# Dividing the spare-bank products of an attention layer over two steps

## The chip, the cores and the metric

The kernel runs on one core of a Trainium2 chip. The metric is the device time of one execution in microseconds (us); the time of a kernel is the median of several runs. TensorE is called PE in the profile, VectorE DVE, ScalarE ACT, GpSimd POOL and SyncE SP.

## The reference

A graph-attention layer with residual normalization, in float32, on x of shape 8 x 2048 x 256 and a 2048 x 2048 adjacency matrix that is shared by all eight frames and all heads (8 heads of 32 channels):

```
q, k, v = split(x @ w_qkv)
scores  = where(adj > 0, q k^T / sqrt(32), -1e9)
t       = softmax(scores) @ v
y       = layernorm(x + t) * g1 + be1
h       = relu(y @ w1 + b1)
z       = layernorm(y + h @ w2 + b2) * g2 + be2
out     = layernorm(x + z)
```

## The kernel before

**Items.** The main loop (L513) goes over 8 frames x 4 query chunks (qc, 512 rows each) x 2 head groups (g, four heads each) x 16 key blocks (mb, 128 keys each): 1024 items. In what follows a frame is 128 steps of this loop, a group is the 16 steps of one (qc, g), and G0 to G7 are the groups of a frame. For each item the scores of four heads are formed transposed, with keys on the partitions (`scores`, L204 to L219): four float32 matmuls of 512 columns into two of three pairs of PSUM banks, then two VectorE additions of the mask (L218), each from one pair into half of an SBUF tile `p`. ScalarE takes exp in place (L222), PE sums values over the 16 key blocks in one PSUM bank (L234), and the denominators are gathered by GpSimd additions (L256) and accumulating DMAs (L253) of the `p` tiles, and by products with a matrix of ones (L292).

**Order.** The program order of every engine is written by hand; nothing is reordered afterwards. One pass t of the loop issues: fill work (`advance`, L526, not at mb 0), the exponentials of item t+1, the scores of item t+2, the values of item t, the additions of item t.

**Banks.** Eight PSUM banks: six in three pairs for scores, two (`ps_x`) that change sides with every group: one holds the running values, the other is the spare bank for fill work. All fill products and transposes inside the loop go through this one bank, each evicted by ScalarE or VectorE before the next may write.

**Fill work.** Everything else is written as Python generators that yield between pieces: the transposes of x and the query projections of a coming frame (`turn`, L155; `queries`, L142; through DRAM, since the transposed chunk is written to `XD` and reloaded later), the reload (`reload`, L177) and the K and V projections of a chunk (`project`, L186; `channels`, L169, makes one 128 x 512 projection of two matmuls with the contraction halved), the denominator of a group (L280), the division (`divide`, L321), and the tail (L333) with the feed-forward (L386) and two further normalizations (`norm`, L259).

A generator yields `BANK` when it wants the spare bank, a number n when it may go on n steps later, and other negative marks for other resources: input tiles (`INPUTS`, three tiles in turn, L110 to L119), the `turned` tile, and room for a tail (two at a time). `advance(t, 1)` (L428) goes over the entries of `fill`, sorted by due time (L422), and runs each one until it has to wait; one piece in a step gets the bank:

```
                if e[2] == BANK:
                    if not banks:
                        break
                    banks -= 1
```

The table `NEXT` (L453) says at which step of a frame the turns and projections of the following frame are started. A reload's `yield 3` (L183) leaves three steps between its DMA and its first product; a K projection waits until all K projections before it exist (L189). If the V of a coming item is missing, the loop L533 calls `advance` until it is there. After the last item the remaining generators are run one after the other (L543).

**Pieces that the change touches.** A projection of Q or K (L172, two matmuls of 512 columns), a value projection (L197, eight matmuls of 128 columns), a first feed-forward product (L405, two matmuls of 512 columns), a second one (L415, four matmuls of 256 columns), and the ones-product (L292), which already runs in two pieces, half of its terms in each, with a second `yield BANK` (L289) between them. Float32 matmuls appear in the profile as two instructions each.

Of the kernel before, what the change touches and what calls it, by code (L numbers as in the profile page):

```python
# [10 lines left out]
F32 = mybir.dt.float32  # L11
# [8 lines left out]
P = 128  # L20
H = 8
D = 32
CH = 512
# [3 lines left out]

SUM_MIN = 1e-25
SUM_MAX = 1e19
BANK, TURNED, ROOM, INPUTS = -1, -2, -3, -10  # L30

MASKED = -57344.0
CODE = -5.0
# [22 lines left out]
def fast_path(ctx, tc, cst, x, adj, out, RS):  # L56
    nc = tc.nc
    F, N, C = x.shape
    NCK, TPC, MB = N // CH, CH // P, N // P
# [17 lines left out]
    ctx.enter_context(tc.manual_schedule())  # L77

    ident, identb, wqkv, w1s, w2s = cst["ident"], cst["identb"], cst["wqkv"], cst["w1s"], cst["w2s"]
    state = {"pair": 0, "side": None, "turn": 0, "turned": False, "tails": 0}  # L80

    def score_pair():
        i = state["pair"]
# [55 lines left out]
    QT, KT, V, XT = {}, {}, {}, {}  # L139
    XD = [dp.tile([NCK, P, 2, CH], F32, name=f"xd{f}") for f in range(F)]  # L140

    def queries(f, c, xT):  # L142
        for g in range(2):
            yield BANK
            QT[f, c, g] = channels(qp, "qT", xT, g * P)

    def turn_rows(xc, xT):
        for a in range(2):
# [17 lines left out]
        yield from queries(f, c, xT)  # L166
        give(xT)

    def channels(pool, name, xT, k0):  # L169
        ps = bank()  # L170
        for a in range(2):
            nc.tensor.matmul(ps, wqkv[:, a, k0:k0 + P], xT[:, a, :], start=(a == 0), stop=(a == 1))  # L172
        t = pool.tile([P, CH], F32, name=name)
        nc.scalar.copy(t, ps)
        return t

    def reload(f, c):  # L177
        while (f, c) not in XT:
# [7 lines left out]
    def project(f, c, g, xT=None):  # L186
        if xT is None:
            xT = yield from reload(f, c)
            while len(KT) < (2 * f + g) * NCK + c:  # L189
                yield 1  # L190
        yield BANK
        KT[f, c, g] = channels(kp, "kT", xT, C + g * P)
        yield BANK
        ps = bank()
        for j in range(TPC):
            for a in range(2):
                nc.tensor.matmul(ps[:, j * P:(j + 1) * P], xT[:, a, j * P:(j + 1) * P],  # L197
                                 wqkv[:, a, 2 * C + g * P:2 * C + (g + 1) * P], start=(a == 0), stop=(a == 1))
        v = vp.tile([P, TPC, P], F32, name="v")
        nc.scalar.copy(v, ps.rearrange("p (j c) -> p j c", c=P))  # L200
        V[f, c, g] = v
        give(xT)
# [21 lines left out]
    LAST = MB - 1  # L224
# [55 lines left out]
    def denominator(f, qc, g):  # L280
        grp = (f, qc, g)
        terms = [PT.pop((f, qc, g, ALONE))] + [PT.pop((f, qc, g, chain[0])) for chain in MOVED + (POOLED,)]
        if (f, qc, g) == items[-1][:3]:
            terms[3:3] = [PT.pop((f, qc, g, b)) for b in ENDED]
        yield BANK
        ps = bank()
        for n, term in enumerate(terms):
            if n == 2:
                yield BANK  # L289
            for h in range(4):  # L290
                r = D * h
                nc.tensor.matmul(ps[r:r + D, :], cst["ones"], term[:, h, :], start=(n == 0), stop=(n == len(terms) - 1))  # L292
        dT = op.tile([P, CH], F32, name="dT")
        nc.scalar.copy(dT, ps)  # L294
        yield 1
        yield BANK
        ps = bank()
        for j in range(TPC):
            nc.tensor.transpose(ps[:, j * P:(j + 1) * P], dT[:, j::TPC], ident)
        if g == 0:  # L300
            RC[f, qc] = op.tile([P, TPC, H], F32, name="rc")
        rc = RC[f, qc]
        den = ps.rearrange("p (j c) -> p j c", c=P)[:, :, ::D]
        nc.vector.reciprocal(rc[:, :, 4 * g:4 * g + 4], den)
        nc.vector.tensor_tensor(RS[:, 0], RS[:, 0], den, ALU.add)
        nc.vector.tensor_tensor(RS[:, 1], RS[:, 1], den, ALU.min)
        if g == 1:
            begin = items.index((f, qc, g, LAST)) + SUM + 2
            start(begin, outcome(f, qc) if (f, qc) != (F - 1, NCK - 1) else finish(f, qc), begin)
# [76 lines left out]
    def feed_forward(y):  # L386
        yield TURNED
        state["turned"] = True
        yT = work.tile([P, 2, CH], F32, name="turned")
        for a in range(2):  # L390
            yield BANK
            ps = bank()
            for j in range(TPC):
                nc.tensor.transpose(ps[:, j * P:(j + 1) * P], y[:, j, a * P:(a + 1) * P], ident)  # L394
            nc.scalar.activation(yT[:, a, :], ps, AF.Identity, bias=cst["be1c"][:, a:a + 1], scale=cst["g1c"][:, a:a + 1])
        yield 1
        nc.gpsimd.tensor_tensor(y, y, rows(cst["g1r"]), ALU.mult)
        yield 1
        nc.gpsimd.tensor_tensor(y, y, rows(cst["be1b2r"]), ALU.add)
        hT = work.tile([P, 2, CH], F32, name="hT")  # L400
        for d in range(2):
            yield BANK
            ps = bank()
            for a in range(2):
                nc.tensor.matmul(ps, w1s[:, a, d * P:(d + 1) * P], yT[:, a, :], start=(a == 0), stop=(a == 1))  # L405
            nc.scalar.activation(hT[:, d, :], ps, AF.Relu, bias=cst["b1s"][:, d:d + 1], scale=1.0)
        state["turned"] = False
        yield 1
        z = y
        for jj in range(0, TPC, 2):  # L410
            yield BANK
            ps = bank()
            for j in range(jj, jj + 2):
                for d in range(2):
                    nc.tensor.matmul(ps[:, (j - jj) * C:(j - jj + 1) * C], hT[:, d, j * P:(j + 1) * P], w2s[:, d, :],  # L415
                                     start=(d == 0), stop=(d == 1))
            nc.vector.tensor_tensor(z[:, jj:jj + 2, :], ps.rearrange("p (b c) -> p b c", c=C), z[:, jj:jj + 2, :], ALU.add)
# [7 lines left out]

    def advance(t, banks):  # L428
        inputs = True
        for e in list(fill):  # L430
            while e[0] <= t:
                if e[2] == BANK:
                    if not banks:
                        break
                    banks -= 1
                elif e[2] < INPUTS:
                    inputs = inputs and not any(u is not None for u in live[:INPUTS - e[2]])
                    if not inputs:
                        break
                elif e[2] == TURNED and state["turned"] or e[2] == ROOM and state["tails"] == 2:  # L440
                    break
                e[2] = next(e[1], None)
                if e[2] is None:
                    fill.remove(e)
                    break
                if e[2] > 0:
                    e[0] = t + e[2]

    items = [(f, qc, g, mb) for f in range(F) for qc in range(NCK) for g in range(2) for mb in range(MB)]
    LEAD = 2  # L450
# [62 lines left out]
    for t, (f, qc, g, mb) in enumerate(items):  # L513
# [9 lines left out]
            state["rows"] = take([P, TPC, C], F32)  # L523
            nc.sync.dma_start(state["rows"], x[f, qc * CH:(qc + 1) * CH, :].rearrange("(p j) c -> p j c", p=P))
        if mb:
            advance(t, 1)  # L526

        if t + 1 < len(items):
            exponentials(items[t + 1])
        if t + LEAD < len(items):  # L530
            nf, _, ng, nmb = items[t + LEAD]
            t0 = t
            while (nf, nmb // TPC, ng) not in V:  # L533
                advance(t0, 1)
                t0 += 1
            scores(items[t + LEAD])
        values(items[t])
# [4 lines left out]
    state["side"] = None  # L542
    while fill:  # L543
        t += 1
        advance(t, 1)


@with_exitstack
# [233 lines left out]
```

## Time and profile before

| | us |
|---|---|
| median of 3 runs | 3436.56 (3432.72 to 3441.2) |
| the profiled execution's own time | 3440.89 |
| its span, first to last instruction | 3439.1 |
| PE busy | 3179.1 (92%) |
| VectorE busy | 2731.0 (79%) |
| GpSimd busy | 2586.7 (75%) |
| ScalarE busy | 2426.5 (71%) |
| first scores of the loop / last scores | 56.0 / 3377.7 after the start |

A line of the page's groups names the source line, the engine, the operation, what it writes and reads, the count, the busy time, the mean duration in ns, and the idle time of the engine before it with what ended it. A line of the timeline gives start, duration, engine, line and operation, `x8` for eight instructions merged, and in brackets the idle time before it. A line of the waits gives who waited for whom: total us, number of times, longest. PEld is PE's weight load. Ends of matmuls are modelled, starts are recorded. Tiles named `s` are the score pairs, `x` the two other banks, `p` the exponentials, `in` the input tiles, `xd` the transposed chunks in DRAM.

### The profile page before, as it was taken

To read this page: it belongs to the slowest core of one execution; us is meant where nothing else is said; L and a number is where in the kernel's file an instruction comes from. 1 tells how busy PE (TensorE), PEld (TensorE's weight loads), DVE (VectorE), ACT (ScalarE), POOL (GpSimd) and SP (SyncE) were. 2 spreads that over 40 slices of the span, in tenths; PEclk is the share of its full clock that TensorE was granted. 3 is DMA by queue.
4 is the path that set the end of the run, shared out by engine and by line. 5 is a ranking of instruction groups with operands and counts; after the bars stand their busy time and mean duration, and the time that the engine had idled before them with its cause. 6 is when DMAs were issued, how large, how long until landed. Compare 5 with 4: busy or idle time off the path is not lost. (4 is left out here: it accounts for less than half of the span.)

```text
span 3439.1 us, 54435 instructions
## 1 busy us (share of the span) xinstructions
PE 3179.1 (92%) x22036; PEld 1038.5 (30%) x22036; DVE 2731.0 (79%) x3203; ACT 2426.5 (71%) x1937; POOL 2586.7 (75%) x1357
## 2 busy tenths in 40 slices
PE   6989999999999999999999999999999999998995
PEld 5222332223322233222332323223332223322222
DVE  4788768887788877888788887888768887689885
ACT  3677767776677767777677776777767777677774
POOL 0577768887688776888678876787777877788885
PEclk8999999999999999999999999999999999999998
DMA  8678768778678777778777777687776787777774
GB/s 309 149 156 173 173 161 174 158 159 200 142 167 184 154 180 153 163 172 181 170 154 170 161 175 178 141 180 172 164 179 140 160 187 167 169 158 154 151 162 99
DMA packets 149298, 575.99 MB, mean 167 GB/s; under 512 B 14608, under 2 KB 67344, under 8 KB 99888
## 3 DMA queue, kind: packets, MB, share of 16 engines
q0 software_dynamic: 64560, 435.85, 63.2%
q1 hardware_dynamic: 83664, 135.30, 11.4%
q8 instruction: 174, 2.85, 0.3%
q10 hardware_dynamic: 816, 1.31, 0.1%
q14 instruction: 84, 0.69, 0.1%
HBM read 131.99 MB, written 37.75 MB: 49 GB/s over the span
## 5 line engine op out<-in xcount | busy, mean ns | idle before, releaser
L218 DVE TENSOR_TENSOR p<-s,mask 128x1024 f32<-128x1024 f32 x2048 | 2410.0, 1219 | 568.5 <-PE s L215 343.9
L222 ACT ACTIVATE p<-p 128x2048 f32<-128x2048 f32 x1024 | 1956.6, 1911 | 484.6 <-DVE p L218 371.2
L256 POOL TENSOR_TENSOR p<-p 128x2048 f32<-128x2048 f32 x382 | 1851.8, 4898 | 385.9 <-ACT p L222 383.4
L215 PE MATMUL s<-qT,kT 32*128 32x512 f32 x8192 | 1169.8, 641 | 184.9 <-DVE p L218 174.6
L234 PE MATMUL x<-p,v 128*32 128x512 f32 x8192 | 1091.8, 605 | 2.3 <-ACT p L222 2.3
L253 POOL DMA_DIRECT2D p<-p x384 | 385.6, 1024 | 376.0 <-DMA p<-p 188.4
L215 PEld LDWEIGHTS s<-qT,kT 32*128 32x128 f32 x8192 | 320.5, 183 | 822.3 <-DVE p L218 756.2
L234 PEld LDWEIGHTS x<-p,v 128*32 128x32 f32 x8192 | 161.1, 108 | 780.1 <-issue 211.5
L172 PE MATMUL x<-in,wqkv 128*128 128x512 f32 x472 | 235.2, 621 | 14.7 <-DMA in<-xd 14.1
L292 PE MATMUL x<-p,ones 128*32 128x512 f32 x2064 | 244.9, 592 | 1.9 <-DMA p<-p 1.9
L274 ACT ACTIVATE y<-y,nb,rs 128x256 f32<-128x256 f32 x372 | 219.0, 590 | 7.1 <-POOL nb L271 7.1
L263 DVE BATCH_NORM_STATS2 st<-y 128x6 f32<-128x256 f32 x372 | 155.4, 418 | 0.0
L172 PEld LDWEIGHTS x<-in,wqkv 128*128 128x128 f32 x472 | 80.2, 189 | 170.9 <-issue 112.7
L294 ACT COPY dT<-x 128x512 f32<-128x512 f32 x64 | 37.4, 585 | 126.3 <-PE x L292 126.3
L415 PE MATMUL x<-w2s,hT 128*128 128x256 f32 x504 | 125.5, 392 | 0.1
L405 PE MATMUL x<-turned,w1s 128*128 128x512 f32 x248 | 123.0, 618 | 0.0
L197 PEld LDWEIGHTS x<-wqkv,in 128*128 128x128 f32 x896 | 104.2, 191 | 47.0 <-issue 41.1
L197 PE MATMUL x<-wqkv,in 128*128 128x128 f32 x896 | 114.9, 281 | 0.0
L292 PEld LDWEIGHTS x<-p,ones 128*32 128x32 f32 x2064 | 66.8, 110 | 156.4 <-issue 151.0
L415 PEld LDWEIGHTS x<-w2s,hT 128*128 128x128 f32 x504 | 90.6, 189 | 62.0 <-issue 50.3
L268 POOL TENSOR_TENSOR rs<-rs,mhalf 128x4 f32<-128x4 f32 x93 | 96.2, 1035 | 7.8
L200 ACT COPY v<-x 128x512 f32<-128x512 f32 x58 | 33.9, 585 | 93.6 <-PE x L197 93.6
(114 smaller groups left out, 1467.6 us busy)
## 6 DMA issues: line engine op xcount, KB each, us to landing
p<-p POOLq DMA_DIRECT2D x384, 1024.0 KB, 10.1
mask<-md SPq DMA_DIRECT2D x248, 128.0 KB, 6.2
y<-in_x_dram POOLq DMA_DIRECT2D x62, 512.0 KB, 6.1
in<-xd SPq DMA_DIRECT2D x59, 512.0 KB, 10.9
p<-in_adj_dram SPq DMA_DIRECT2D x16, 1024.0 KB, 9.6
out_dram<-y SPq DMA_DIRECT2D x31, 512.0 KB, 6.4
in<-in_x_dram SPq DMA_DIRECT2D x29, 512.0 KB, 10.4
xd<-in SPq DMA_DIRECT2D x28, 512.0 KB, 9.2
```

The costliest lines, as they stand in the source:

```text
L172: nc.tensor.matmul(ps, wqkv[:, a, k0:k0 + P], xT[:, a, :], start=(a == 0), stop=(a == 1))
L197: nc.tensor.matmul(ps[:, j * P:(j + 1) * P], xT[:, a, j * P:(j + 1) * P], wqkv[:, a, 2 * C + g * P:2 * C + (g + 1) * P], start=(a == 0), s ...
L215: nc.tensor.matmul(ps2[half][:, j, :], KT[f, mb // TPC, g][r:r + D, (mb % TPC) * P:(mb % TPC + 1) * P], QT[f, qc, g][r:r + D, :], start=Tr ...
L218: nc.vector.tensor_tensor(pt[:, 2 * half:2 * half + 2, :], ps, MK[f, qc, mb // 2][:, mb % 2, None, :].to_broadcast([P, 2, CH]), ALU.add)
L222: nc.scalar.activation(PT[item], PT[item], AF.Exp, scale=1.0 / math.sqrt(D))
L234: nc.tensor.matmul(O[grp][r:r + D, :], V[f, mb // TPC, g][:, mb % TPC, r:r + D], PT[item][:, h, :], start=(mb == 0), stop=(mb == LAST))
L253: nc.gpsimd.dma_start(PT[f, qc, g, chain[0]], PT.pop(item), accum_op=ALU.add)
L256: nc.gpsimd.tensor_tensor(first, first, PT.pop(item), ALU.add)
L263: nc.vector.bn_stats(st, t[:, j, :])
L274: nc.scalar.activation(t[:, j, :], t[:, j, :], AF.Identity, bias=nb[:, j:j + 1], scale=rs[:, j:j + 1])
L292: nc.tensor.matmul(ps[r:r + D, :], cst["ones"], term[:, h, :], start=(n == 0), stop=(n == len(terms) - 1))
L415: nc.tensor.matmul(ps[:, (j - jj) * C:(j - jj + 1) * C], hT[:, d, j * P:(j + 1) * P], w2s[:, d, :], start=(d == 0), stop=(d == 1))
```

## The change

Projections, value projections and both feed-forward products get a new mark, `MORE`, in their middle. A job that has yielded `MORE` becomes the holder of the bank: the next call of `advance` resumes it first and gives the bank to nobody else. If, at the end of the call in which it stopped, another entry is due and waits for `BANK`, the holder is resumed at once, so that its product is issued whole. The calls at mb 15, in the loop that waits for a V, and after the last item finish the holder in any case. The ones-product's second `yield BANK` becomes `HOLD`, which keeps the bank for the next step whether others wait or not. `channels` becomes a generator that stores its result itself.

```diff
     def queries(f, c, xT):
         for g in range(2):
-            yield BANK
-            QT[f, c, g] = channels(qp, "qT", xT, g * P)
+            yield from channels(QT, qp, "qT", (f, c, g), xT, g * P)
...
-    def channels(pool, name, xT, k0):
+    def channels(store, pool, name, key, xT, k0):
+        yield BANK
         ps = bank()
         for a in range(2):
+            if a:
+                yield MORE
             nc.tensor.matmul(ps, wqkv[:, a, k0:k0 + P], xT[:, a, :], start=(a == 0), stop=(a == 1))
-        t = pool.tile([P, CH], F32, name=name)
-        nc.scalar.copy(t, ps)
-        return t
+        store[key] = pool.tile([P, CH], F32, name=name)
+        nc.scalar.copy(store[key], ps)
...
-        yield BANK
-        KT[f, c, g] = channels(kp, "kT", xT, C + g * P)
+        yield from channels(KT, kp, "kT", (f, c, g), xT, C + g * P)
         yield BANK
         ps = bank()
         for j in range(TPC):
+            if j == TPC // 2:
+                yield MORE
             for a in range(2):
...
             if n == 2:
-                yield BANK
+                yield HOLD
...
             for a in range(2):
+                if a:
+                    yield MORE
                 nc.tensor.matmul(ps, w1s[:, a, d * P:(d + 1) * P], yT[:, a, :], start=(a == 0), stop=(a == 1))
...
             for j in range(jj, jj + 2):
+                if j > jj:
+                    yield MORE
                 for d in range(2):
...
+    def resume(e, t):
+        e[2] = next(e[1], None)
+        state["holder"] = e if e[2] in (MORE, HOLD) else None if state["holder"] is e else state["holder"]
+        if e[2] is None:
+            fill.remove(e)
+        elif e[2] > 0:
+            e[0] = t + e[2]
+
-    def advance(t, banks):
+    def advance(t, free=True, finish=False):
         inputs = True
+        if state["holder"]:
+            free = False
+            resume(state["holder"], t)
         for e in list(fill):
-            while e[0] <= t:
+            while e[2] is not None and e[0] <= t and e is not state["holder"]:
                 if e[2] == BANK:
-                    if not banks:
+                    if not free:
                         break
-                    banks -= 1
+                    free = False
...
-                e[2] = next(e[1], None)
-                if e[2] is None:
-                    fill.remove(e)
-                    break
-                if e[2] > 0:
-                    e[0] = t + e[2]
+                resume(e, t)
+        late = any(e[2] == BANK and e[0] <= t for e in fill)
+        while state["holder"] and (finish or late and state["holder"][2] == MORE):
+            resume(state["holder"], t)
...
         if mb:
-            advance(t, 1)
+            advance(t, finish=mb == LAST)
...
             while (nf, nmb // TPC, ng) not in V:
-                advance(t0, 1)
+                advance(t0, finish=True)
                 t0 += 1
...
     while fill:
         t += 1
-        advance(t, 1)
+        advance(t, finish=True)
```

More of the change, by code (lines that the diff above doesn't have):

```diff
@@ L29 @@
 SUM_MAX = 1e19
-BANK, TURNED, ROOM, INPUTS = -1, -2, -3, -10
+BANK, MORE, HOLD, TURNED, ROOM, INPUTS = -1, -2, -3, -4, -5, -10
 MASKED = -57344.0
@@ L79, in fast_path @@
     ident, identb, wqkv, w1s, w2s = cst["ident"], cst["identb"], cst["wqkv"], cst["w1s"], cst["w2s"]
-    state = {"pair": 0, "side": None, "turn": 0, "turned": False, "tails": 0}
+    state = {"pair": 0, "side": None, "turn": 0, "turned": False, "holder": None, "tails": 0}
     def score_pair():
```

## The prediction

> **What bounds the kernel now.** I read the page first (busy shares, groups), then the timeline of single steps, then the waits and the DMA issues. "Step t" is one pass of the loop over items: fill work of L526, exponentials of item t+1, scores of t+2, values of t. There are 1024 (L222's count), 128 to a frame, in groups G0 to G7 of 16; "mb" is a step's place in its group.
>
> ```profile
> PE 3179.1 (92%) x22036; PEld 1038.5 (30%) x22036; DVE 2731.0 (79%) x3203; ACT 2426.5 (71%) x1937; POOL 2586.7 (75%) x1357
> ...
> L172 PE MATMUL x<-in,wqkv 128*128 128x512 f32 x472 | 235.2, 621 | 14.7 <-DMA in<-xd 14.1
> ...
> L415 PE MATMUL x<-w2s,hT 128*128 128x256 f32 x504 | 125.5, 392 | 0.1
> L405 PE MATMUL x<-turned,w1s 128*128 128x512 f32 x248 | 123.0, 618 | 0.0
> ...
> L197 PE MATMUL x<-wqkv,in 128*128 128x128 f32 x896 | 114.9, 281 | 0.0
> ```
>
> PE leads, but 92% is an average over two kinds of step. The counts give the products that use the spare bank inside the loop: 472/4 = 118 projections (L172), 248/4 = 62 first and 504/8 = 63 second feed-forward products, 896/16 = 56 value projections, 299 in all. First a step without fill work, in the timeline (start, length, then the idle time before it):
>
> ```profile
> 1473.41 1.14 PE L215 MATMUL s<-qT,kT 32*128 32x512 f32 x8 [0.41 <-DVE p L218]
> ...
> 1474.48 1.07 PE L234 MATMUL x<-p,v 128*32 128x512 f32 x8
> ...
> 1474.67 2.35 DVE L218 TENSOR_TENSOR p<-s,mask 128x1024 f32<-128x1024 f32 x2 [0.19 <-issue]
> 1475.95 0.31 PEld L215 LDWEIGHTS s<-qT,kT 32*128 32x128 f32 x8 [1.32 <-DVE p L218]
> 1475.95 1.14 PE L215 MATMUL s<-qT,kT 32*128 32x512 f32 x8 [0.41 <-DVE p L218]
> ```
>
> Scores to scores is 2.54 us. PE's own work is 1.07 (scores to values) plus 1.00 (values to whatever is next, 1507.71 to 1508.71 below), 2.07; the other 0.47 it waits for VectorE's mask add, which frees the pair that the next scores overwrite. Now a step with a whole projection:
>
> ```profile
> 1506.64 1.14 PE L215 MATMUL s<-qT,kT 32*128 32x512 f32 x8
> ...
> 1507.71 1.06 PE L234 MATMUL x<-p,v 128*32 128x512 f32 x8
> ...
> 1507.85 2.36 DVE L218 TENSOR_TENSOR p<-s,mask 128x1024 f32<-128x1024 f32 x2 [0.76 <-PE s L215]
> ...
> 1508.71 0.30 PEld L172 LDWEIGHTS x<-in,wqkv 128*128 128x128 f32 x2 [0.84 <-ACT y L274]
> 1508.71 1.98 PE L172 MATMUL x<-in,wqkv 128*128 128x512 f32 x4
> 1509.24 0.19 PEld L172 LDWEIGHTS x<-in,wqkv 128*128 128x128 f32 x1 [0.24 <-issue]
> 1509.67 0.19 PEld L172 LDWEIGHTS x<-in,wqkv 128*128 128x128 f32 x1 [0.24 <-issue]
> 1510.62 0.31 PEld L215 LDWEIGHTS s<-qT,kT 32*128 32x128 f32 x8 [0.76 <-DVE p L218]
> ```
>
> This one takes 3.98 us, PE never waits, and VectorE idles some 1.6. So PE bounds the full steps and the loop PE-VectorE the empty ones: 0.47 us of PE is unused in each empty step. Starts of the matmul groups, sorted over the whole loop, give 357 empty steps (median 2.544), 64 of them at mb 0, where no fill work is called. Two waits belong to single places:
>
> ```profile
> DVE y L417 <- POOL y L399: 22.3, 13, 3.7
> ...
> PE x L172 <- DMA in<-xd: 14.1, 8, 3.1
> ```
>
> **What the Trainium skill says.** "TensorE: Matmul & The Clock Gate", Part 3, The mechanism: matmuls start and end strictly in program order. The trace agrees: every step's groups start in the code's order, so a product put before the scores delays them by its length. "Perfetto Trace Analysis", Tensor Engine Instruction: the reported end of a matmul is an estimate. The trace agrees (1506.64 + 1.14 lies behind the next start, 1507.71), so I use starts alone. "PSUM — Partial Sum Buffer", The four PSUM rules: a matmul that opens a sum clears flags only in its own bank; an open sum can stay while others run in other banks. The ones-products (L288) already do so here at 3.78 us for each of their steps. "DMA: Bandwidth & Descriptors", Issuing engines are not separate DMA queues: SP's and GpSimd's transfers share 16 engines. It agrees: the 512 KB reload `in<-xd` lands 10.9 us after its issue in the median, but 3.2 to 16.9 us in single issues, shortest where no accumulating `p<-p` is under way.
>
> **The change, part by part.** *Price of one division.* In the full step PE's starts are 0.53, 0.43, 0.43 and 0.52 us apart (two passes to each matmul), 1.91 in all. A half is 0.53 + 0.52 = 1.05, so a divided pair of steps is 2 x (2.07 + 1.05) = 6.24 us against 3.98 + 2.54 = 6.52: **0.28 us gained**. L405 has the same starts, and L415 (0.32 + 2 x 0.216 + 0.31 a half) and L197 (0.21 + 6 x 0.112 + 0.20) come to 0.28 too. The half step needs cover: VectorE has 2.36 plus 0.65 where a row statistic falls in, 3.0 of 3.12; ScalarE 1.91 (exp) + 0.59 (eviction) + 0.59 (normalize) = 3.1, just full, but such steps come singly.
>
> *How many.* A job is divided only if no other one waits for the bank, and not at mb 15. I took the order of the fill jobs from the trace (frames 1 to 6 are alike) and walked it by hand under the new rule: C projection, V values, h and z the feed-forward's two, o ones, d/r/x/y transposes, + the second half of the job before it, a dot no fill work.
>
> ```
>      before            after                before            after
> G0   .zVoodrr........  .zzoodrrVC+VC+VC  G4 .zCoodrrV.......  .hzzoodrrV+.....
> G1   ...oodxxCCyy.hhz  .V+oodxxC+Cyy.h+  G5 ...oodxxCCyyChhz  ...oodxxC+CyyC+h
> G2   .z.oodrr........  .h+zzoodrr......  G6 .zVoodrrxxCCCVCV  .hzzoodrrxxCCV+.
> G3   ...oodxxCCyy.hhz  ...oodxxC+CyyC+h  G7 .CVoodCVCVyyChhz  .C+oodVC+VyyC+hh
> ```
>
> Most jobs stay whole because a second job is queued: the later z halves meet the waiting ones-product, the V's the next chunk's K. 15 per frame are divided; frame 0 has 13 (no tails yet), frame 7 has 10 (no projections of its own): 6 x 15 + 13 + 10 = **113**. Sum: 113 x 0.28 = **31.6 us less**. The rest of the empty steps stays empty (17 of 32 usable per frame).
>
> *What moves with it.* All jobs keep their work, but jobs slip by up to nine steps, with the evictions, row statistics and DMAs that follow them.
> - Second feed-forward product: today its eviction waits at mb 15 for GpSimd's additions (22.3 us of VectorE waits above); in trace steps G4 mb 0 is 0.86 us longer than an empty step and G6's 0.23. The product comes one to four steps later, the additions at most one. Gain about 1.1 a frame, 7 in all.
> - Row statistics after it (L263, 0.65 us each) slip from the ones steps, where VectorE idles, into d and r steps, where it is full (r steps are 0.11 over their PE length already). Up to 0.6 in each of G2, G4, G6 and 0.3 in G0, less 1.2 taken out of x steps and empty steps of G1, G3, G5: about +1 a frame, 7 in all, against the gain before it.
> - Reloads on SP's queue. Today the fourth chunk's K projection (G6 mb 14) waits 0 to 4.6 us, 2.2 on average, for its reload, which waits for its own write to DRAM; it now comes at G7 mb 7, with time to spare. In its place: the second chunk's V (due later than all others) moves from G6 mb 2 to mb 13 and 14 and holds its input tile till then, so the third chunk's reload, until now issued as early as G5 mb 15 to G6 mb 12, is issued only at its end. Its K projection starts two empty steps and one scores-values later, 0.2 + 2 x 2.54 + 2.07 = 7.4 us. At 7 to 11 us for a first reload in that stretch (8.1 to 10.6 for those issued at G6 mb 12) PE waits 0 to 3.6; I take 2. The first chunk's reload (issued G3 mb 8, landing after 15 to 17 us) is needed 15.2 us later: 0.6 more. Together +0.4 a frame; bounds -2 and +3, or -15 and +20 over seven frames. Behind PE's wait stand the scores and so all engines. The mask loads that SP has queued are for the next query chunk, not due.
> - ones-products slip by two steps in G2, one in G4 and G6; the `p` tiles they hold have 11 buffers and no wait of VectorE for GpSimd's sums shows.
> - The end (61 us after the last scores) is bound by the last sums and gets one second product more, 2 us beside their transfers: 0.
>
> These four shifts cancel to within about 10 us; I take 0. The profiled execution took 3440.9 us (span 3439.1, 1.8 around it), so 3409 for one like it; it was 4.3 above the median of the three runs. From the median: 3436.6 - 31.6 = **3405 us**.
>
> **Rivals.**
> A, *slower*: the third chunk's reload. If it lands S us after PE is ready, the time is 3405 + 7 x (S - 2); from S = 6.5 (a landing after 13.9 us) there is no gain. For it: other reloads take 13 to 17 us behind mask loads or as third in a row. Against: this one is first in the queue, with the last accumulation of its group ending. At 16 us S is 8.6 and the time 3451.
> B, *half steps are not PE-bound*: ScalarE's 3.1 us and VectorE's moved statistics make a pair 6.4 rather than 6.24: 113 x 0.14 = 16, time 3421. For it: both engines are within 4% of the half step. Against: only one in three halves carries such an extra.
> C, *hardly anything is divided*: if my walk misses waiting jobs and only the places with long empty runs behind them count (G1 to G4, about 50 in all): 14 us, time 3423.
> D, *all usable empty steps are filled*: 293 x 0.28 = 82, time 3355. Against: the queued jobs above; bursts and empty runs lie in different groups.
>
> **How the numbers follow.** Forecast 0.72, B 0.11, C 0.07, A 0.06, D 0.04. The forecast's own spread is about 12 us (reloads, statistics, 10 divisions more or fewer = 3 us, the median's own scatter of 4): 3393 to 3417. Up to 3426 it takes in B and C, and leaves A, D and the tails out: 3393 to 3426. About 0.3% (10 us) is what a measurement of this kernel can tell from no change, so faster means below 3426: 0.71 + 0.09 + 0.05 + 0.04 = 0.89, which I lower to 0.86 for what I have not seen; same 0.09; slower 0.05.
>
> **What would show it.** Right: about 113 pairs of steps at 3.12 us with two L172 or L405 passes each; some 113 fewer empty steps; L215's wait for L218 shorter; G6 mb 14 at 3.1 us with half a V; a wait `PE x L172 <-DMA in<-xd` at G7 mb 1 instead of G6 mb 14. Wrong: half steps above 3.2 us (B), far fewer divided products (C), or that DMA wait above 6 us a frame (A).

## The result, and the profile after

| | before | after |
|---|---|---|
| median of 4 runs each, side by side | 3435.72 us (3432.72 to 3441.2) | 3436.27 us (3430.64 to 3437.18) |
| ratio | | 0.9996, 95% interval 0.9979 to 1.0014 |
| profiled execution, own time | 3440.9 us | 3435.6 us |
| its span | 3439.1 us | 3433.5 us |

No change that the measurement can tell, where 31.6 us less were forecast. Run again beside the kernel before on a second chip (below) the changed kernel stood at 0.998 (0.9969 to 0.9991), some 6 us less. So the question is where 26 to 32 us went.

From the page of after, the busy shares and the group of the Q and K projections:

```profile
PE 3205.3 (93%) x22036; PEld 1035.0 (30%) x22036; DVE 2736.9 (80%) x3203; ACT 2427.4 (71%) x1937; POOL 2588.2 (75%) x1357
...
L174 PE MATMUL x<-in,wqkv 128*128 128x512 f32 x472 | 257.3, 643 | 21.0 <-DMA in<-xd 17.2
```

The counts of instructions are the same, and the means are no guide, as ends are modelled. The wait ahead of L174 for `in<-xd` rose from 14.1 to 17.2 us (one more wait for it, 3.8 us in frame 4, is put down to ScalarE). A divided projection in the timeline of after:

```profile
1908.35 1.14 PE L217 MATMUL s<-qT,kT 32*128 32x512 f32 x8
1909.42 1.06 PE L236 MATMUL x<-p,v 128*32 128x512 f32 x8
1910.41 1.13 PE L174 MATMUL x<-in,wqkv 128*128 128x512 f32 x2
1911.47 1.14 PE L217 MATMUL s<-qT,kT 32*128 32x512 f32 x8
1912.54 1.06 PE L236 MATMUL x<-p,v 128*32 128x512 f32 x8
1913.53 1.13 PE L174 MATMUL x<-in,wqkv 128*128 128x512 f32 x2
1914.59 1.14 PE L217 MATMUL s<-qT,kT 32*128 32x512 f32 x8
```

Scores to scores is 3.12 us twice, PE without a gap: the half step is what the prediction said. To see the rest I gave every step of the two profiled executions the length that it has where nothing disturbs it (empty 2.54, whole projection 3.98, half 3.12, and so on, from the timelines) and summed what each kind takes beyond that, from the scores of item 17 to those of item 1022. The kinds have the letters of the prediction's walk: C a projection, h and z the feed-forward's two products, o the ones-product, d, r, x and y transposes.

| us | before | after |
|---|---|---|
| undisturbed lengths | 3169.6 | 3138.9 |
| beyond them: C steps | 16.6 | 32.7 |
| r steps | 6.7 | 23.5 |
| x and y steps | 8.1 | 3.5 |
| empty steps | 27.7 | 17.0 |
| others | 1.4 | 0.8 |
| sum of these steps | 3230.2 | 3216.4 |
| all steps, first to last scores | 3321.6 | 3305.2 |
| last scores to the end | 61.5 | 72.1 |

So PE's part of the gain is there, 30.7 us in these steps (113 divided products, every one in the row where the prediction put it). It is given back in two places: at places 13 and 14 of G3, where 31.6 of the C steps' 32.7 us lie, and at the end, which is 10.7 us longer. (The C steps' 16.6 us of before lay elsewhere, 15.0 of them at G6 place 14, and are gone; the 17 us that the r steps took more are nearly made up by the 15 that the x, y and empty steps took less.) G3 place 13 in frame 1, in the timeline of after:

```profile
687.73 1.10 PE L174 MATMUL x<-in,wqkv 128*128 128x512 f32 x2 [3.11 <-DMA in<-xd]
688.75 1.62 PE L217 MATMUL s<-qT,kT 32*128 32x512 f32 x8
690.31 1.93 PE L236 MATMUL x<-p,v 128*32 128x512 f32 x8
692.17 1.36 PE L174 MATMUL x<-in,wqkv 128*128 128x512 f32 x2
693.47 1.14 PE L217 MATMUL s<-qT,kT 32*128 32x512 f32 x8
```

PE waits for the first chunk's reload, and then works slowly: from these scores to the values it takes 1.56 us and from the values to the next product 1.86, where 1.07 and 0.99 are usual. The windows of the same stretch show the granted clock (columns: stretch, length, busy us of PE, PEld, DVE, ACT and POOL with their instructions, then clock, DMA share, GB/s):

```profile
684.00:688.00 4.00, 0.89 (x9) 0.30 (x2) 2.36 (x3) 3.09 (x2) 2.36 (x2) 1.00 1.11 260
688.00:692.00 4.00, 4.00 (x18) 0.51 (x16) 1.52 (x2) 0.36 (x1) 3.58 (x2) 0.66 1.02 234
```

PE pauses at this place in all seven frames, for 1.6 to 3.8 us. With each of the five pauses of 2.8 us and more comes a clock record of 0.5, which begins near the end of the pause and lasts 3.4 or 6.8 us, and the step at place 14 is 1.0 to 2.1 us longer; with the pauses of 1.6 and 2.0 us comes none. The Trainium skill ("TensorE: Matmul & The Clock Gate", Part 1, What's actually happening) says that PE falls to half its rate after an idle window of about 3.4 us; the trace agrees on the half rate, but here pauses that the profile gives as 2.8 to 3.2 us were enough (ends of matmuls are modelled). The column ahead of the last says the second thing: the DMA engines are full there (share 1.02 to 1.11). They were so before, too. By half group of frame 4, places 0 to 7 and 8 to 15 of G3, first in before and then in after:

```profile
1893.00:1917.00 24.00, 22.05 (x172) 6.08 (x172) 21.58 (x32) 17.44 (x13) 23.38 (x14) 1.00 0.55 112
1917.00:1945.00 28.00, 27.55 (x164) 8.94 (x168) 20.90 (x21) 23.14 (x24) 20.30 (x13) 1.00 1.02 237
...
1884.00:1908.00 24.00, 21.69 (x170) 6.02 (x171) 21.12 (x28) 17.39 (x13) 23.08 (x14) 1.00 0.54 114
1908.00:1940.00 32.00, 28.23 (x156) 7.78 (x154) 21.85 (x26) 21.21 (x19) 22.76 (x13) 0.89 1.04 232
```

The kernel before had no product that needed this reload before G4. The divided kernel needs it in the full half group.

The end in after, GpSimd's and SyncE's lines of the timeline: L343 is the be2r addition of the last tail, L345 its transfer, L386 the finish's output, L348 the tail's.

```profile
3413.95 4.76 SPq L386 DMA_DIRECT2D out_dram<-y  x2
3414.82 2.34 POOL L343 TENSOR_TENSOR y<-y,be2r 128x1024 f32<-128x1024 f32 x1
3417.46 0.94 POOL L345 DMA_DIRECT2D y<-in_x_dram  x1 [0.30 <-POOL y L343]
...
3429.59 0.33 SPq L348 DMA_DIRECT2D out_dram<-y  x1
```

Before, these two stood ahead of the finish's second normalization, 36.7 and 39.4 us after the last scores:

```profile
3414.35 2.35 POOL L341 TENSOR_TENSOR y<-y,be2r 128x1024 f32<-128x1024 f32 x1
3417.00 0.92 POOL L343 DMA_DIRECT2D y<-in_x_dram  x1 [0.30 <-POOL y L341]
3418.07 0.19 POOL L359 TENSOR_SCALAR rs<-mv 128x2 f32<-128x2 f32 x1 [0.16 <-DVE mv L357]
```

In after they stand behind all of the finish's GpSimd work, at 53.4 and 56.0, and the tail's output leaves last.

### The profile page after: what moved, and what is told of

It is laid out like the page before. It is cut to its first block, busy times and chain, and to the rows that moved or that the text cites. A ratio compares the mean times of both kernels' runs of the same rounds, so it can differ in the third digit from the quotient of the medians.

```text
span 3433.5 us, 54404 instructions
## 1 busy us (share of the span) xinstructions
PE 3205.3 (93%) x22036; PEld 1035.0 (30%) x22036; DVE 2736.9 (80%) x3203; ACT 2427.4 (71%) x1937; POOL 2588.2 (75%) x1357
## 5 line engine op out<-in xcount | busy, mean ns | idle before, releaser
L258 POOL TENSOR_TENSOR p<-p 128x2048 f32<-128x2048 f32 x382 | 1815.1, 4755 | 311.1 <-ACT p L224 309.7
L255 POOL DMA_DIRECT2D p<-p x384 | 358.4, 989 | 426.0 <-DMA p<-p 201.6
L174 PE MATMUL x<-in,wqkv 128*128 128x512 f32 x472 | 257.3, 643 | 21.0 <-DMA in<-xd 17.2
L174 PEld LDWEIGHTS x<-in,wqkv 128*128 128x128 f32 x472 | 75.0, 191 | 206.1 <-issue 157.5
L176 ACT COPY kT<-x 128x512 f32<-128x512 f32 x59 | 34.5, 585 | 81.0 <-PE x L174 81.0
```

What stands on the lines that cost most here:

```text
L255: nc.gpsimd.dma_start(PT[f, qc, g, chain[0]], PT.pop(item), accum_op=ALU.add)
L258: nc.gpsimd.tensor_tensor(first, first, PT.pop(item), ALU.add)
```

## The experiments

Each run is set against the kernel before on its own chip; that took 3435.7 us on the first chip and 3445 to 3450 on the others, so ratios are compared, and "beyond" means the sums of the table above.

**First theory: the reload in G3 and the end, each by itself.** The reload is asked for four steps later; the last tail's feed-forward (frame 7, third chunk: `whole`) is not divided; both; and, apart from them, only the projections of Q, K and V are divided.

```diff
e1  -(3, 10): [(project, 0, 0)]      +(3, 14): [(project, 0, 0)]
e2  -            if a:               +            if a and not whole:  
    -            if j > jj:          +            if j > jj and not whole:
e3  both
e4  -            if a:  yield MORE   (feed-forward)
    -            if j > jj:  yield MORE
```

> The changed kernel with one number altered: the next frame's first chunk is asked for at G3 mb 14 instead of mb 10, so that its K projection falls to G4 mb 9, far behind the landing of its reload. Theory of the reload (the gain of the halves is real and is lost in PE's wait for that reload and in the slower TensorE clock after it): in the trace of the changed kernel G3 mb 13 and 14 are 5.0 us per frame above their halves' length, so 7 x 5 = 33 us leave: about 3403 us, ratio to before 0.990, no step of that place above 3.2 us. Rival (the row statistics that moved into the division's steps, 16.8 us more there, or halves that cost more than counted, eat the gain): within 5 us of the changed kernel's 3436.

> The changed kernel, with the feed-forward of the last but one query chunk's tail (the one that runs into the end) undivided. Theory of the end: the half that is held over mb 13 and 14 pushes this tail one step behind the final chunk's work, so that its last addition stands behind that chunk's on GpSimd and its last transfer comes alone: the end from the last scores falls from 72 to about 61 us as before, 10 us less in all: about 3426. Rival (the end is longer because the loop ran faster and its sums arrive at the same time): the end stays near 72 us, the time at 3436.

> Both edits together. If the two costs are separate they add: 3436 - 33 - 10 = 3393 us, ratio 0.9875, which is the 31 us of the halves and the loss of the wait that the kernel before has at its fourth chunk. The rivals: 3426 to 3436.

> The changed kernel with both feed-forward products whole again and only projections divided (13 a frame, 94 in all, 26 us by the price of 0.28). The first chunk's K projection stays at G3 mb 13 and the last tail runs as before. Theory: -26 for the halves, +16 for the reload against the waits of before, end as before: 3436 - 10 = 3426. Rival (halves don't pay): 3436 or more.

Measured: e1 3437.8 us, 0.9961 (0.9947 to 0.9976); e2 3436.5, 0.9962 (0.9949 to 0.9975); e3 3435.2, 0.9962 (0.9949 to 0.9976); e4 3441.2, 0.9975 (0.9962 to 0.9988). In e1 the C steps fall from 32.7 to 1.0 beyond, but the h steps rise from 0.4 to 28.0, nearly all at G4 place 1, and the empty ones from 17.0 to 25.0: the wait moved one group on and kept its size. e2 takes 4 of the 10.7 us off the end (68.2). e3 has both effects and gains nothing more. e4, with fewer divisions, keeps 22.5 in the C steps; its 9 us below the kernel before are near the 10 expected. The changed kernel itself had no run on this chip, so whether e1 to e3 gain a few us on it can't be told; the 33 and 43 us that the theory gave to e1 and e3 are out. So the theory fell as stated: the late reload is where the loss shows, not what makes it.

**Second theory: the transfers are late in the odd groups because the DMA engines are full.** Beside the changed kernel itself: two of the six accumulating transfers of each group left out, in the kernel before and in the changed one; and one of GpSimd's six additions of a group left out instead.

```diff
e6, e7  -                nc.gpsimd.dma_start(PT[f, qc, g, chain[0]], PT.pop(item), accum_op=ALU.add)
        +                term = PT.pop(item)
        +                if mb != chain[-1]:
        +                    nc.gpsimd.dma_start(PT[f, qc, g, chain[0]], term, accum_op=ALU.add)
e8      -            nc.gpsimd.tensor_tensor(first, first, PT.pop(item), ALU.add)
        +            term = PT.pop(item)
        +            if mb != 11:
        +                nc.gpsimd.tensor_tensor(first, first, term, ALU.add)
```

> The changed kernel itself, without an edit, so that it shares a chip with the three runs beside it and with the kernel before. Nothing is to be told apart by it alone. Every theory expects what its first profile showed: C steps (those with a projection of keys) 30 to 34 us above their PE length, nearly all of it at places 13 and 14 of G3 in frames 1 to 6, 72 us from the last scores to the end, and a ratio to the kernel before of 0.996 to 1.000.

> The kernel before with the last accumulating transfer of each of the two chains left out (places 10 and 12 of every group: those two p tiles are dropped, so the denominator lacks them), 4 MB moved per group in place of 6. My theory, that late transfers set the time in the second half of the odd groups (their share of the DMA engines is 0.95 to 1.04 there): the wait at G6 place 14 goes (16 us), 3424 to 3434 if the kernel before takes 3440, and the chip's ratio is 0.994 to 0.998. Rival, that the transfers' amount has no part in it: within 4 us of the kernel before.

> The changed kernel with the same two accumulating transfers of each group left out (places 10 and 12, so the denominator lacks them). My theory: with room on the DMA engines the first chunk's reload comes in time and nothing takes its place, C steps at most 8 us above their PE length and no stall at G4 places 0 and 1; the loop is 28 to 34 us shorter than that of the kernel before with the same two left out, and what is left of the loss is the end alone (7 to 11 us), so its time is 18 to 27 us below that run's. Rival, that the stalls have another cause (order of the queues, the reload's own length): C steps 25 us or more above their PE length as in the changed kernel, and only 0 to 10 us below that run.

> The changed kernel with one of GpSimd's six additions of each group left out instead (the p tile of place 11 is dropped, so the denominator lacks it), all transfers kept: GpSimd has 4.7 us more in each group. My theory, that it is the DMA engines: the stalls of G3 stay, C steps 20 us or more above their PE length, time within 8 us of the changed kernel. Rival, that GpSimd's own work in order (additions ahead of the issue of the next transfer and of the small operations of a normalization) is the limit: C steps below 10 us above their PE length, waits of ScalarE for nb of L273 below 8 us (25 in the changed kernel), time 15 to 30 us below the changed kernel.

Measured: e5 3440.0 us, 0.998 (0.9969 to 0.9991); e6 3417.4, 0.9921 (0.9901 to 0.9941); e7 3405.4, 0.9887 (0.9867 to 0.9908); e8 3437.7, 0.9975 (0.9965 to 0.9985). e5, the same kernel as after, has 36.8 us in its C steps, one wait of 8.0 us among them, so a few us there are scatter. With fewer transfers the C steps fall to 0.5 in the kernel before and 5.0 in the changed one; the first reload of G3 lands after 12.2 to 16.4 us in e7, 16.2 to 23.0 in e5. e6 gained more than expected (0.9921 against 0.994 to 0.998). The second half of G3 in e7, frame 4:

```profile
1898.00:1924.00 26.00, 26.00 (x156) 7.15 (x153) 21.33 (x25) 20.95 (x20) 21.18 (x12) 1.00 0.79 187
```

Share 0.79, clock 1.00, PE busy throughout. The loop of e7 is 20.4 us shorter than that of e6, short of the 28 to 34 expected, since the r steps (23.3 against 6.7) were still long, and its end 10.3 us longer, as between the kernels themselves; so the whole is 12 us shorter, where 18 to 27 were expected and the rival gave 0 to 10. It is the C steps, not the time, that tell the two apart. In e8 GpSimd turned part of its free time into waiting for the transfers. Its waits for `p<-p`, in total us, times and longest, in e5:

```profile
POOL p L255 <- DMA p<-p: 220.9, 57, 7.8
```

and the same line of the waits of e8:

```profile
POOL p L255 <- DMA p<-p: 349.6, 73, 10.5
```

The time didn't move beyond the intervals and 34.9 us stayed in the C steps. So the amount of transfers, not that of GpSimd's additions, makes the reload late.

**What follows a late feed-forward.** The last tail no longer gives way ahead of its addition and transfer (e9); the four row statistics after the second feed-forward product are issued two to a step, in the two steps after it (e10); the first chunk's projection is asked for in G2 (e11); all three (e12).

```diff
e9   (in tail, last = the tail of frame 7, third chunk; twice)
     -        yield 1
     +        if not last:
     +            yield 1
e10  -            yield 1
     +            if j % 2 or not pairs:
     +                yield 1
     (pairs: the second normalization of a tail)
e11  -(3, 10): [(project, 0, 0)]      +(2, 9): [(project, 0, 0)]
e12  all three
```

> The changed kernel, in which the last tail (frame 7, third query chunk) no longer gives way for a step ahead of its be2r addition and ahead of the transfer that adds x, so both are queued on GpSimd ahead of the finish's second and third normalization, as they were in the kernel before. My theory of the end, that 10.7 us are lost there since that tail comes a step later and its transfer then stands behind the finish's GpSimd work: 60 to 64 us from the last scores to the end (72.1 in the changed kernel, 61.5 before), time 8 to 12 us below the changed kernel, loop unchanged. Rival, that the end is longer since the last sums' transfers land late and everything follows from that: 69 us or more, time within 3 us.

> The changed kernel, in which the four row statistics after the second feed-forward product are issued two to a step in the two steps that follow it (the ones-products, where VectorE idles 1.4 us of 3.78) in place of one to a step in four. Theory, that these 0.65 us operations made the r steps 16.8 us longer (6.7 before, 23.5 after): r steps 4 to 10 us above their PE length. Then two outcomes. If PE's and VectorE's lengths add up to the loop, the loop is 13 to 17 us shorter than the changed kernel's. Rival, that the accumulating transfers set when the odd groups' second halves pass, so that what is saved in G2's r steps is lost again at the reload in G3: C steps grow by as much (40 us or more above their PE length), and the loop is at most 8 us shorter.

> The changed kernel with the first chunk's projection asked for in G2 at place 9 (in place of G3, place 10), so that its reload goes out in an even group, where the DMA engines' share is 0.5 to 0.9 in place of 1.0, and the 512 KB (some 2.6 us of all 16 engines at the share that the accumulating transfers take) leave G3's second half. My theory, transfers late in the odd groups: no wait for this reload, C steps below 10 us above their PE length, and at least half of G3's 5 us a frame does not come back at G4 place 1, so the loop is 15 to 30 us shorter than the changed kernel's. Rival, that GpSimd's accumulations are late there without the reload too: the loss comes back at G4 places 0 and 1 or in h, z and empty steps, as when the reload was put later, and the time is within 5 us of the changed kernel.

> The three edits together: last tail in order, statistics in pairs, first chunk's reload in G2. If each does what my theory expects of it (end 10 us, r steps 15, reload 15 to 30), 40 to 55 us below the changed kernel; if the transfers of the odd groups take back what the others save, 10 to 20 below (the end and little more).

Measured: e9 3433.8 us, 0.9961 (0.9945 to 0.9976); e10 3391.5, **0.9842** (0.9821 to 0.9862); e11 3429.2, 0.9948 (0.9929 to 0.9967); e12 3369.2, **0.9773** (0.9753 to 0.9794).
- e9: 64.8 us from the last scores to the end. The order of GpSimd's queue is 7 of the 10.7 us. The loop of the profiled execution was 7 us longer than that of after, with 40 us in its C steps, so the ratio doesn't show the gain by itself.
- e11: this reload causes no wait any more, as the theory said, but C steps are 15.8 beyond, now at G5, and h and d steps some 13 more. The wait moved again; the loop is 3 us shorter, where the theory gave 15 to 30.
- e10: far more than either theory gave it (the loop is some 43 us shorter than that of after, where 13 to 17 and at most 8 were expected). The r steps are at their undisturbed length, the C steps at 13.1, and the end is 62.2 us. What an r step looked like in after (frame 4, G2 place 9): a statistic and the division's product ahead of the mask add, for which the next scores wait. VectorE has 0.41 + 0.18 + 0.67 + 2.34 us to do in a step in which PE has 2.75:

```profile
1866.49 0.41 DVE L265 BATCH_NORM_STATS2 st<-y 128x6 f32<-128x256 f32 x1
1866.94 0.18 DVE L266 BATCH_NORM_AGGREGATE mv<-st 128x2 f32<-128x6 f32 x1
1867.04 0.67 DVE L331 TENSOR_TENSOR y<-x,rc 128x512 f32<-128x512 f32 x1
1867.63 2.34 DVE L220 TENSOR_TENSOR p<-s,mask 128x1024 f32<-128x1024 f32 x2
```

- e12: all waits beyond the undisturbed lengths are down to 23.8 us. By the ratios it is 71 to 77 us below the changed kernel (0.998 and 0.9996), where 40 to 55 were expected; most of what it has more comes with the pairs.

**What the pairs did.** The same edit in the kernel before (e13); in the changed kernel with the rest of the tail held for two steps (e14); e10 again (e15); and the kernel before with pairs and the fourth chunk's turn asked for sooner, which removes its own wait at G6 place 14 (e16).

```diff
e13  e10's edit in the kernel before
e14  e10's edit, and after the four statistics
     +        if pairs:
     +            yield 2
e16  e13's edit, and -(6, 0): [(turn, 3)]   +(5, 12): [(turn, 3)]
```

> The kernel before, with the row statistics after the second feed-forward product issued in pairs as in the run with statistics in pairs. Theory, that the halves' gain was eaten by statistics which the change moved into the r steps: the kernel before has little of that (r steps 6.7 us above their PE length), so it gains 5 to 12 us, and the changed kernel with the same edit lies 30 to 45 us below it. Rival, that pairs are a gain of their own which has nothing to do with the division: it gains 30 to 48 us as the changed kernel did, and the two with pairs lie within 10 us of each other.

> The changed kernel with statistics in pairs, but the rest of that tail (GpSimd's small operations, the normalization, additions and transfers) held for two steps, so that it comes as late as in the changed kernel. If the r steps alone made the difference: r steps at their PE length, C steps as with pairs (about 13 us above), 3390 to 3396 if the run with pairs beside it takes 3391. If it is the tail's coming two steps sooner, with its GpSimd work and transfers, that lets the first chunk's reload come in time and shortens the end: C steps 30 us or more above their PE length, 70 us or more from the last scores to the end, and 20 to 30 us longer than the run with pairs.

> The changed kernel with statistics in pairs once more, so that the three runs beside it have it on their chip. Both theories expect what it showed: 3385 to 3395, 0.982 to 0.986 of the kernel before.

> The kernel before with statistics in pairs and the fourth chunk's turn asked for four steps sooner (G5 place 12 in place of G6 place 0), which removes its own wait for a reload at G6 place 14 (16.6 us). Theory, that what the division is worth is its PE time once the waits on both sides are gone: 15 to 25 us below the kernel before, so still 25 to 35 us above the changed kernel with pairs. Rival, that the kernel before gains as much from such edits as the changed one: within 10 us of the changed kernel with pairs.

Measured: e13 3529.3 us, **1.0241** (1.0224 to 1.0258); e14 3421.2, 0.9929 (0.9913 to 0.9946); e15 3391.7, 0.984 (0.9822 to 0.9859); e16 3464.1, 1.0048 (1.0029 to 1.0066).
- e15 repeats e10, with 19.7 us in the C steps against 13.1.
- e14 against e15: with the r steps free but the tail as late as in the changed kernel, the C steps are at 33.9 again (19.7 in e15) and the end at 73.4 (62.0). So of the gain of pairs about 22 us are the r steps themselves (the table's steps take 3219.3 in e5, on another chip, and 3197.2 in e14), and 28 us the tail's two steps: 17 in the loop, 11 at the end.
- e13 took 84 us more than the kernel before, where one theory expected 5 to 12 less and the other 30 to 48 less. Its o steps are 77.1 us beyond, and its waits say why:

```profile
DVE p L218 <- DMA p<-p: 84.7, 37, 5.1
```

The kernel before has 3.0 us there. VectorE's mask add waits for an accumulating transfer to land before it writes its `p` tile. Lines of GpSimd and VectorE around the start of G3 in frame 4, in e13's timeline (L344 is the tail's transfer, L253 the group's last accumulating one), and below them GpSimd's two in that of before, where the order is the other one (L343 is the tail's transfer):

```profile
1942.75 1.18 POOL L344 DMA_DIRECT2D y<-in_x_dram  x1
1943.32 1.50 POOL L253 DMA_DIRECT2D p<-p  x1
...
1954.00 2.36 DVE L218 TENSOR_TENSOR p<-s,mask 128x1024 f32<-128x1024 f32 x2 [3.61 <-DMA p<-p]
```

```profile
1893.07 1.19 POOL L253 DMA_DIRECT2D p<-p  x1
...
1900.50 1.52 POOL L343 DMA_DIRECT2D y<-in_x_dram  x1
```

With the tail two steps sooner, its transfer is queued ahead of the last accumulation, which lands 10.56 us after its issue (7.50 in before), and the mask add at place 3 of the next group waits for that. e16, expected 15 to 25 us below the kernel before, came out 19 above: its earlier turn removed the wait that it was meant for (C steps 0.0), but 51.9 us stayed in the o steps. The order of the two transfers I tested by holding that one transfer for a step (e17), and with the turn's edit too (e18):

```diff
e17  e13's edit, and ahead of the tail's last transfer
     -        yield 1
     +        yield 2
e18  e16's edit and the same
```

> The kernel before with statistics in pairs and only the tail's last transfer (the one that adds x after the second normalization) held for one step more. Theory of why pairs cost the kernel before 84 us: with the tail two steps sooner this transfer goes onto GpSimd's queue ahead of the group's last accumulating transfer, which then lands 5 us late in the next group's place 3, where the ones-products wait for it (77 us of o steps). Held for a step it goes behind it again: o steps at most 10 us above their PE length, time 0.992 to 1.006 of the kernel before. Rival, that it is the earlier additions and small operations on GpSimd, not the transfer's place: o steps stay 50 us or more above, 1.015 or more of the kernel before.

> The kernel before with statistics in pairs, that transfer held for a step and the fourth chunk's turn four steps sooner: all waits that I know of in the kernel before taken away, for a comparison of the division with those waits gone on both sides. Theory, that the division is worth its PE time there: 0.986 to 0.994 of the kernel before, so 8 to 14 thousandths (28 to 48 us) above the changed kernel with its own three edits (0.977). Rival, that orders of GpSimd's queue decide and the division has little worth: 0.983 or less.

Measured: e17 3463.3 us, 1.0048 (1.0031 to 1.0064), o steps 1.2 beyond. The order of the two transfers is the cause of the 77 us; the wait of the mask add for `p<-p` is down from 84.7 to 18.6 us in e17. (The expectation said that the ones-products wait; the trace shows that it is the mask add.) What remains in e17 is above all the wait at G6 place 14, 33.2 of the C steps' 39.0 us. e18, without that: 3423.8 us, 0.9927 (0.9912 to 0.9942).

e18 and e15 ran on one chip and say what the division is worth when each kernel's other waits are about equal: 40.7 and 41.5 us beyond, undisturbed lengths 3169.6 and 3138.9, ends 63.7 and 62.0, medians 3423.8 and 3391.7. That is **32 us** (30 by the ratios), against 31.6 in the prediction's sum. The two differ by more than the division (e18 has the earlier turn and the held transfer, too), so this is an account that comes out even and not a test of one edit. The expectation had named e12 for this comparison: that lies 53 us below e18 by the ratios, where 28 to 48 were expected; 17 us fewer waits are left in it.

## Why the prediction was wrong

- *Price and number of divisions* (0.28 us, 113): right. The rows of the loop are those written down, the half steps 3.12 to 3.16 us, the undisturbed lengths 30.7 us less. Rivals B, C and D are out.
- *Second feed-forward product and row statistics* (-7 and +7): both right. The waits at place 0 of G4 and G6 fell from 6.5 us to nothing; r and y steps rose by 19 and x and other empty steps fell by 11, 8 together.
- *Third chunk's reload* (2 us a frame, 14 in all): nothing was lost; no wait shows at G7 place 1. Rival A is out. The fourth chunk's 15 us went as said. This error of 14 us has the other sign and by luck hides half of the next one.
- *First chunk's reload* ("0.6 more", about 4 us): **this step failed**; places 13 and 14 of G3 lost 31.6 us. It stood on a landing after 15 to 17 us and a need after 15.2. The need was about right: PE was ready 14.7 to 15.1 us after the issue (the start of place 13's values plus their 1.0 us). The landing was not: it came after 16.2 to 18.8 us, 17.7 on average where before had 16.0, and PE paused 19.8 us in the seven frames. And the term had nothing for what follows a pause: PE's slower work after five of them cost some 12 us more, 1.0 us in place 13 of frames 4 to 6 and the rest mostly in place 14.
- What made the landing late: I had taken the landing time of before as a property of the transfer. In e7, with a third of the accumulating transfers left out, it is 14.7 us on average and the C steps lose 5.0. In e15 and e14, which differ in the two steps by which the tail is held, it is 17.1 and 18.0, PE pauses 15.7 and 22.3 us, and a clock record of 0.5 follows in two frames and in six. So it depends on the traffic and on where the tails stand in it. By which way the slipped jobs delay it is not shown. The shares of G3's halves are as before (above), and the tail's transfer, now at place 4 of G3 in place of 2 or 3, lands some 7 us ahead of the reload's issue. What did change is the half group before G3: its share fell from 0.99 to 0.73 in frame 4, and the first of the tail's two last additions moved from it into G3.
- *The end* (0): **failed** too, 10.7 us. I costed the product that moves behind the last item by its own 2 us and not by what is queued behind it: the tail's last transfer fell behind the finish's work on GpSimd (e9: 7 us of it; e2: 4 us by keeping that product ahead).
- *"These four shifts cancel to within about 10 us"*: the bound was set from the sizes of the moved operations. What they move in turn was left out: in e13 a shift of every tail by two steps costs 84 us. The errors of the terms, 28 - 14 + 11, come to 25 us; the profiled execution of after took 27 us more than the 3409 that the prediction gave for it.

The Trainium skill ("DMA: Bandwidth & Descriptors", SWDGE vs HWDGE vs iDMA) says that a transfer which accumulates must come from GpSimd. The trace agrees: all 384 `p<-p` and 62 `y<-in_x_dram` are on GpSimd's queue, among 382 additions of 4.76 us. So sums and tails share one order, and e9 and e17 show what a changed place in it costs.

What stays open: by which way the slipped jobs delay the first chunk's reload; why it still waits in e10 and e15 by amounts that differ from frame to frame (places 13 and 14 lose 0.1 to 6.2 us); why the wait at G6 place 14 grew from 15.0 us to 39.4 in e13 and 33.2 in e17; and 3.3 of the end's 10.7 us, left in e9 (64.8 against 61.5): the finish's own output starts 53.5 us after the last scores there and 50.2 in before, which was not taken apart.

## What to carry to other kernels

Where a small saving is spread over many steps, cost not only the operations that slip but the queue in which their followers stand: list, for each slipped job, which of its transfers passes which other one on the issuing engine, and in which stretch it now runs. A landing time read from a trace holds only for the traffic that the trace had; where the DMA engines are at their limit, a moved reload moved the wait and left the sum of the waits as it was (e1, e11), and only less or better placed traffic made it smaller (e7, e10). Then look for the cheap repair: here issuing four 0.6 us statistics in two steps instead of four, one order at the end and one earlier reload took the changed kernel from no gain to 0.977 of the kernel before.

## What was not expected of the hardware

- A PE pause of about 3 us costs more than itself: in after five pauses of 2.8 to 3.8 us, 16 us in all, came with a granted clock of 0.5 and some 12 us of slower work, two of 1.6 and 2.0 us without. Between 2.4 and 2.8 us it went both ways: 2.8 us in frame 5 of e10 and of e15 without it, 2.4 in frame 4 of e15 with it.
- Leaving a third of the accumulating transfers out made the kernel before 0.8% faster although no row of its waits of VectorE or ScalarE for them holds more than 3.0 us. Beside GpSimd's own waits for them (188.4 us in before), their load shows in other transfers' landing times (G3's first reload 14.9 to 17.0 us in before, 10.5 to 15.5 without them) and so in waits put down to those (C steps 16.6 to 0.5).
